# A segment-mean graph layer: gathers of 128 successive edges, with a one-hot in a band of 32 columns

## The chip, the cores and the metric

The kernel runs on one core of a Trainium2 chip. Its time is the device time of one execution in microseconds (us). The runs before give a median of 25,311.82 us (three runs, 25,302.51 to 25,315.38). One execution was taken by the hardware profiler; all rows and lines shown are from it.

## The reference

100,000 nodes with 64 features each, and 3,300,000 edges `(src, dst)`, sorted by `dst`. Of the edges 3,200,000 have random ends (1,600,000 pairs in both directions) and 100,000 are self loops, so a node has 33 edges on the mean, and at least one.

```
h = maximum(layernorm(x), 0)
y = concat([h[dst], h[src] - h[dst]]) @ W.T + b          # one row per edge
out = x + segment_sum(y, dst) / max(count(dst), 1)
```

The matrix product is linear, so the kernel needs for each node only the sum of `h[src]` over its edges and their number; the product with W is done on nodes.

## The kernel before

**First stage** (0 to about 430 us). The normalized features `h` are written to HBM as three bf16 parts that add up to the float32 value, with two columns of ones behind: a row of `h3` has 194 bf16 numbers. The tensor `acc` (a row of 64 sums and a count per node) is set to zero. The function `bounds` (line 249) reads the `dst` numbers of the chunks (see below) and finds for each chunk the least and the greatest node.

**Sorted sets.** The first 2,039,808 edges (256 lists of 7,968) are sorted on VectorE and ScalarE by source node (436 to some 2,500 us for most of it), and are then summed without gathers: for every stretch of 640 nodes a table of `h3` rows is loaded, and TensorE picks rows from it by a one-hot `gh` (line 806) and adds them up by a one-hot `dh` (lines 828 and 836). There are 64 sets; 4 run in a straight part and 60 in a loop of 3 turns with 20 sets each (line 944).

**Chunks.** The last 1,260,192 edges are cut into 352 chunks of 3,584 edges (`CHUNK` = 128 x `J`, `J` = 28). 351 are full; the last has 2,208 edges and 1,376 fills, whose source is node 0 and whose `dst` is V = 100,000, a row behind the last node. Each chunk takes 28 gathers: GpSimd's indirect DMA fetches 128 rows of `h3`, one per partition, into `nb` (line 403). A one-hot `hot` says for each of the 128 gathered rows to which of the 128 nodes from the chunk's least node on it belongs; VectorE writes it for 14 gathers in one instruction (`one_hot`, line 345), by comparing `near`, the node number relative to the least one, four times repeated, with the numbers 0 to 127. TensorE adds up the chunk with 28 matmuls (line 408) into one PSUM tile `ps`, VectorE reduces it to `sums` (lines 420 and 422), and SP stores it in `acc`. In the arrays `src_p` and `dst_p` a chunk has the shape 128 x 28, so that gather `j` takes the edges `j`, `j + 28`, `j + 56` and so on, and partition `p` holds 28 successive edges. The instructions of the chunks are interleaved by hand with those of the sets: 70 chunks with the sort and the first 4 sets, 94 with each turn of the main loop.

**Flags.** The sums in `acc` hold only if the data meet some conditions: a chunk spans under 128 nodes, a list spans under 256 nodes, and so on. Each condition writes a flag into the tensor `odd`. At the end the greatest of all flags is taken (`worst`, line 990), and the two counts in `turns` come from it (lines 995 and 996): `n_clear`, 0 or 1, and `n_slow`, 0 or `NF` = 1,612. They are the number of turns of two loops that follow:

- Line 1004: 28 DMAs set `acc` to zero.
- Line 1014: each turn takes 2,048 edges of the whole list, in the order of the list, sorted or in chunks alike. It loads their numbers (`si`, `di`, and `dr`, which is `dst` in all partitions), gathers 16 times 128 rows (line 1024), compares all `dst` within each gather (`same`), adds up equal ones by a matmul (line 1042), and adds the sums into `acc` with 16 indirect DMAs that accumulate (line 1046). Rows that are not the first of their node go to rows behind the last node.

Before these loops three accumulating stores (line 960) and five accumulating indirect DMAs (line 971) add to `acc` what chunks and lists share at their ends. **Last stage:** the mean, the product with W, and `out` (lines 1057 to 1086).

The part of `bounds` that the change touches, before:

```
nc.vector.tensor_reduce(least[:n, m:m + 1], d[:n], axis=AX.X, op=ALU.min)
if m == NMT - 1:
    nc.vector.scalar_tensor_tensor(d[:n], d[:n], float(V), d[:n], op0=ALU.is_lt, op1=ALU.mult)
nc.vector.tensor_reduce(most[:n, m:m + 1], d[:n], axis=AX.X, op=ALU.max)
```

`NMT` is 3: the chunks are looked at in groups of 128, 128 and 96, one chunk per partition. The multiplication in the last group sets the fills' numbers to 0.

Of the kernel before, what the change touches and what calls it, by code (L numbers as in the profile page):

```python
# [13 lines left out]
F32 = mybir.dt.float32  # L14
BF16 = mybir.dt.bfloat16
I32 = mybir.dt.int32
I16 = mybir.dt.int16
AF = mybir.ActivationFunctionType
ALU = mybir.AluOpType
AX = mybir.AxisListType  # L20
# [7 lines left out]
P = 128  # L28
P = 128
EPS = 1e-5  # L30
J = 28
CHUNK = P * J
# [5 lines left out]
JH = 14  # L38
LAG = 3
GATHER = 1250  # L40
STEP = 1300
GAP = 4
EARLY = 3
EXTRA = 350
KEEP = 5
# [16 lines left out]
D = 4  # L62
# [35 lines left out]
def gnn_preln(ctx: ExitStack, tc, x, src_w, dst_w, src_p, dst_p, src_a, dst_a, wT, b, out, V, E):  # L98
# [17 lines left out]
    nc = tc.nc  # L116
# [3 lines left out]
    CE = C3 + 1  # L120
# [14 lines left out]
    NMT = -(-NCH // P)  # L135
# [27 lines left out]
                   allow_small_or_imprecise_dtypes=True)  # L163
# [7 lines left out]
    for i in range(2):  # L171
# [7 lines left out]
                   allow_small_or_imprecise_dtypes=True)  # L179
# [9 lines left out]
    odd = consts.tile([P, 4 + 5 * LANES], F32, name="odd")  # L189
# [12 lines left out]
    with tc.tile_pool(name="c16s", bufs=1) as c16s:  # L202
        c16_s = c16s.tile([P, REACH + CH], I16, name="c16_s")
        nc.gpsimd.iota(c16_s[:, :REACH].rearrange("p (b s) -> p b s", b=NR), pattern=[[P, NR], [0, P]], base=0,
                       channel_multiplier=1)
# [6 lines left out]
    with tc.tile_pool(name="pre", bufs=2) as pre, tc.tile_pool(name="small", bufs=4) as small, \  # L212
# [13 lines left out]
        for r in range(R, RT, P):  # L226
            n = min(P, RT - r)
# [14 lines left out]


        least = small.tile([P, NMT], F32, name="least", bufs=1)
        most = small.tile([P, NMT], F32, name="most", bufs=1)
        nc.vector.memset(least, 0.0)
        nc.vector.memset(most, 0.0)

        def bounds(m):
            n = min(P, NCH - m * P)  # L250
            d = pre.tile([P, CHUNK], I32, name="d")
            nc.sync.dma_start(d[:n], dst_p[m * P:m * P + n].rearrange("c p j -> c (p j)"))
            nc.vector.tensor_reduce(least[:n, m:m + 1], d[:n], axis=AX.X, op=ALU.min)
            if m == NMT - 1:

                nc.vector.scalar_tensor_tensor(d[:n], d[:n], float(V), d[:n], op0=ALU.is_lt, op1=ALU.mult)
            nc.vector.tensor_reduce(most[:n, m:m + 1], d[:n], axis=AX.X, op=ALU.max)
            if m < NMT - 1:
                return
            span = small.tile([P, NMT], F32, name="span", bufs=1)  # L260
            nc.vector.tensor_sub(span, most, least)
            nc.vector.tensor_reduce(odd[:, 0:1], span, axis=AX.X, op=ALU.max)
            nc.vector.tensor_scalar(odd[:, 0:1], odd[:, 0:1], float(P), None, op0=ALU.is_ge)
            l_ps = pre_ps.tile([NMT, P], F32, name="l_ps")
            nc.tensor.transpose(l_ps, least, ident)
            l_f = small.tile([NMT, P], F32, name="l_f", bufs=1)
            nc.vector.tensor_copy(l_f, l_ps)
            l_i = small.tile([NMT, P], I32, name="l_i", bufs=1)
            nc.vector.tensor_copy(l_i, l_ps)
            nc.sync.dma_start(base_i, l_i)  # L270
            nc.sync.dma_start(base_r, base_i.rearrange("m p -> (m p)")[None, :])
            nc.sync.dma_start(base_f, l_f)
            nc.sync.dma_start(base_b, base_f.rearrange("m p -> (m p)")[None, :].to_broadcast([P, NMT * P]))


        for t in range(0, NPT, T):
# [22 lines left out]
            for u in range(0, T, SUB):  # L299
                n = min(SUB, T - u)  # L300
# [18 lines left out]
    with tc.tile_pool(name="rows", bufs=6) as rows, \  # L319
# [20 lines left out]
        def add_now(all_of_them=False):  # L340
            while later and (all_of_them or (later[0][0] <= count[0] and count[0] - count[1] >= GAP)):
                later.pop(0)[1]()
                count[1] = count[0]

        def one_hot(out, numbers, n):

            shape = [out.shape[0], out.shape[1], n // D, D]
            nc.vector.tensor_tensor(out.rearrange("p k (a d) -> p k a d", d=D),  # L348
                                    numbers[:, :, None].to_broadcast(shape),
                                    upto[:shape[0], :n].rearrange("p (a d) -> p a d", d=D)[:, None].to_broadcast(shape),  # L350
                                    ALU.is_equal)

        def chunks(first, n, dynamic=None):


            def load(q):
                k = min(KG, n - q)
                at = slice(first + q, first + q + k) if dynamic is None else ds(dynamic + q, k)
                si = index.tile([P, KG, J], I32, name="si")
                nc.sync.dma_start(si[:, :k], src_p[at].rearrange("k p j -> p k j"))  # L360
                di = index.tile([P, KG, J], I32, name="di")
                nc.sync.dma_start(di[:, :k], dst_p[at].rearrange("k p j -> p k j"))
                rel = index.tile([P, KG, J], F32, name="rel", bufs=1)
                nc.vector.tensor_sub(rel[:, :k], di[:, :k], base_b[:, at][:, :, None].to_broadcast([P, k, J]))
                near = index.tile([P, KG, J, D], I16, name="near")
                nc.vector.tensor_scalar(near[:, :k], rel[:, :k, :, None].to_broadcast([P, k, J, D]), float(2 * CH), None,
                                        op0=ALU.min)
                return si, near

            def keep(q, sums):  # L370
                c = ds(first + q if dynamic is None else dynamic + q, 1)
                after = ds(first + q + 1 if dynamic is None else dynamic + q + 1, 1)

                def put():
                    at = number(base_r[0:1, c], SP, V)
                    last[SP] = nc.sync.dma_start(acc[ds(at, P)], sums)

                def shared():
                    at = number(base_r[0:1, after], SP, V)
                    last[SP] = nc.sync.dma_start(side_c[c], acc[ds(at, 1)])  # L380

                add_later((LAG - 1) * J, put)
                add_later((LAG - 1) * J + GAP, shared)

            ahead = load(0)
            before = None
            parts = J // JH
            for k in range(n * parts + 1):
                q, part = divmod(k, parts)
                u = q % KG  # L390
                if q < n:
                    if u == 0 and part == 0:
                        si, near = ahead
                    hot = rows.tile([P, JH, P], BF16, name="hot", bufs=4)
                    nb = rows.tile([P, JH, CT], BF16, name="nb")
                    with behind():
                        one_hot(hot, near[:, u, part * JH:part * JH + JH], P)
                if before is not None and before[2] == 0:
                    ps = rows_ps.tile([P, CE], F32, name="ps")
                for j in range(JH):  # L400
                    if q < n:
                        at = part * JH + j
                        last[POOL] = nc.gpsimd.indirect_dma_start(  # L403
                            out=nb[:, j], out_offset=None, in_=h3,
                            in_offset=bass.IndirectOffsetOnAxis(ap=si[:, u, at:at + 1], axis=0))
                        count[0] += 1
                    if before is not None:
                        nc.tensor.matmul(ps, lhsT=before[0][:, j], rhs=before[1][:, j, :CE],  # L408
                                         start=before[2] == 0 and j == 0, stop=before[2] == parts - 1 and j == JH - 1)
                    if q < n:  # L410
                        add_now()
                        yield
                if u == KG - 2 and part == parts - 1 and q + 2 < n:
                    with behind():
                        ahead = load(q + 2)
                if before is not None and before[2] == parts - 1:
                    own = dynamic is None and before[3] < EARLY
                    sums = (few if own else rows).tile([P, C1], F32, name="early" if own else "sums", bufs=EARLY if own else LAG + 2)
                    with behind():
                        nc.vector.tensor_reduce(sums[:, :C], ps[:, :C3].rearrange("p (s c) -> p c s", s=3),  # L420
                                                axis=AX.X, op=ALU.add)
                        nc.vector.tensor_copy(sums[:, C:], ps[:, C3:])  # L422
                    if own:
                        early.append(sums)
                    else:
                        keep(before[3], sums)
                if q < n:
                    before = (hot, nb, part, q)
            add_now(True)
# [325 lines left out]
        def quads(base, n, kept=None):  # L755
# [110 lines left out]
            def keep(u, i, sums):  # L866
# [11 lines left out]
                add_later((LAG - 1) * J, put)  # L878
                add_later((LAG - 1) * J + GAP, shared)

# [16 lines left out]
        with tc.tile_pool(name="few", bufs=1) as few:  # L897
# [14 lines left out]
            with tc.tile_pool(name="keys", bufs=2) as big, tc.tile_pool(name="piece", bufs=2) as piece, \  # L912
                    tc.tile_pool(name="fill", bufs=2) as fill, tc.tile_pool(name="sort_ps", bufs=2, space=PSUM) as ps:
                for l in range(NL):
                    rest = fill_lane(l - 1, fill, took) if l else iter(())
                    for i, ns in enumerate(sort_lane(l, big.tile([P, WL], F32, name="keys"), piece, few, ps)):
                        k = i - 40
# [8 lines left out]
            with tc.tile_pool(name="load", bufs=3) as load, tc.tile_pool(name="hots", bufs=3) as hots, \  # L926
# [13 lines left out]
                for k in range(0, NTB, KEEP):  # L940
                    m = min(TG, NCB - k * TG)
# [20 lines left out]
    with tc.tile_pool(name="few", bufs=1) as few, tc.tile_pool(name="w_ps", bufs=1, space=PSUM) as wps:  # L962
# [18 lines left out]
        small = few.tile([1, 4], F32, name="small")  # L981
# [26 lines left out]
    with tc.tile_pool(name="any", bufs=2) as edge, tc.tile_pool(name="any_c", bufs=1) as one, \  # L1008
# [3 lines left out]
        before = one.tile([P, P], F32, name="before")  # L1012
        nc.vector.tensor_scalar(before, iota, pcol, None, op0=ALU.is_lt)
        with tc.For_i(0, n_slow, 1) as c:
# [25 lines left out]
            for j in range(JA):  # L1040
                ps = edge_ps.tile([P, CE], F32, name="ps")
# [8 lines left out]
    with tc.tile_pool(name="post", bufs=2) as post, tc.tile_pool(name="post_ps", bufs=2, space=PSUM) as post_ps:  # L1050
# [10 lines left out]
        for t in range(0, NPT, T):  # L1061
# [12 lines left out]
            for u in range(0, T, SUB):  # L1074
                n = min(SUB, T - u)
# [50 lines left out]
```

## Time and profile before

| | us |
|---|---|
| median of three runs | 25,311.82 |
| profiled execution | 25,318.98 |
| its span, first to last instruction | 25,317.3 |
| PE (matmul) busy | 14,841.3 (59%) |
| DVE (VectorE) busy | 11,321.0 (45%) |
| POOL (GpSimd) busy | 10,302.7 (41%) |
| ACT (ScalarE) busy | 6,060.7 (24%) |
| mean granted TensorE clock | 0.723 |

Engines run side by side, each in its own order, and wait for each other by semaphores. A row of the page names the line, the engine, the operation, output and input with their shapes, how often it ran, its busy time, the mean of one in ns, and the idle time of the engine just before it with what ended most of it. A line of the timeline gives the start, the duration, and in brackets the idle time before. "SPq" and "POOLq" are queues of engines that issue DMAs; an issue is not the transfer, which ends later.

### The profile page before, as it was taken

The page shows a single profiled execution, that of the slowest core. Times are in us where ns is not written, and L with a number is a line of the kernel's source. Part 1 is how long each engine was busy: PE and PEld are TensorE (multiplying, and loading weights), DVE is VectorE, ACT ScalarE, POOL GpSimd, SP SyncE. Part 2 cuts the span into 40 slices and gives each one's busy share as a digit, 9 for nine tenths or more (in the row PEclk, how much of TensorE's full clock was granted, in tenths as well). Part 3 has the DMA queues.
Part 4 walks back from the last instruction along what each step waited for, and adds up shares of the span by engine and source line. Part 5 has one row for each costly group of instructions (what it writes and reads, how often), then busy time and mean ns, then how long its engine had stood idle before and what let it go on. Part 6 is the DMA issues. An engine that isn't in the chain of part 4 may idle for free. (4 is left out here: it accounts for less than half of the span.)

```text
span 25317.3 us, 562905 instructions
## 1 busy us (share of the span) xinstructions
PE 14841.3 (59%) x238778; PEld 10732.9 (42%) x238778; DVE 11321.0 (45%) x15478; ACT 6060.7 (24%) x11710; POOL 10302.7 (41%) x10609
## 2 busy tenths in 40 slices
PE   4100365466666666665666666666566666666666
PEld 3000244344444444444444444444444444444445
DVE  6878443243444444443444444444344444444444
ACT  4333221122222222221222222222222222222222
POOL 5666533433333333334333333333333333333334
PEclk6555577677777777777777777777777777777777
DMA  6722354354454454454444544444445444444446
GB/s 227 102 46 46 100 172 147 108 151 143 145 149 145 147 149 143 149 153 134 147 143 147 149 146 148 149 147 145 138 144 148 145 150 146 150 145 145 148 145 231
DMA packets 1671411, 3615.08 MB, mean 143 GB/s; under 512 B 951932, under 2 KB 960263, under 8 KB 1663911
## 3 DMA queue, kind: packets, MB, share of 16 engines
q1 hardware_dynamic: 1225338, 3006.63, 36.6%
q0 software_dynamic: 335040, 507.40, 10.5%
q10 hardware_dynamic: 108492, 64.90, 1.3%
q8 instruction: 1874, 30.70, 0.5%
q14 instruction: 667, 5.46, 0.1%
HBM read 3397.56 MB, written 219.36 MB: 143 GB/s over the span
## 5 line engine op out<-in xcount | busy, mean ns | idle before, releaser
L403 POOL DMA_INDIRECT nb<-h,si x9856 | 9337.3, 947 | 13259.9 <-PE ps L408 8539.2
L348 DVE TENSOR_TENSOR dh<-dt,c 128x1024 bf16<-128x1024 int16 x5056 | 3450.9, 683 | 12561.4 <-remote 7908.4
L830 ACT CAST gs<-gp 128x386 bf16<-128x386 f32 x10048 | 4786.8, 482 | 16980.7 <-remote 9615.5
L836 PE MATMUL total<-gs,dh 32*128 32x193 bf16 x160768 | 6254.9, 264 | 4279.4 <-issue 4266.3
L828 PE MATMUL gp<-tab,gh 128*128 128x193 bf16 x48408 | 6076.5, 270 | 2426.6 <-issue 2187.6
L828 PEld LDWEIGHTS <-gh 128*128 128x128 bf16 x60288 | 5384.1, 105 | 4772.8 <-issue 4394.3
L836 PEld LDWEIGHTS <-dh 32*128 32x128 bf16 x160768 | 3875.8, 99 | 6281.3 <-issue 6228.6
L806 DVE TENSOR_TENSOR gh<-srs,c 128x1536 bf16<-128x1536 int16 x5056 | 4760.5, 942 | 15.0 <-issue 7.9
L408 PE MATMUL ps<-nb,hot 128*128 128x193 bf16 x9856 | 1934.7, 281 | 2839.1 <-DVE sums L422 1230.1
L408 PEld LDWEIGHTS <-hot 128*128 128x128 bf16 x9856 | 1048.8, 111 | 3031.1 <-DVE sums L422 1261.7
L828 PE MATMUL gp<-kept,gh 128*128 128x193 bf16 x11880 | 1551.9, 274 | 505.0 <-issue 493.1
L470 ACT COPY tmp<-keys 128x1536 f32<-128x1536 f32 (+14 forms) x540 | 649.6, 1212 | 1324.0 <-DVE keys L472 602.4
L348 DVE TENSOR_TENSOR hot<-near,c 128x1792 bf16<-128x1792 int16 x704 | 759.5, 1079 | 113.6 <-remote 107.4
L471 DVE TENSOR_TENSOR keys<-tmp,keys 128x1536 f32<-128x1536 f32 (+14 forms) x540 | 756.6, 1420 | 88.8 <-ACT junk L548 41.4
L472 DVE TENSOR_TENSOR keys<-tmp,keys 128x1536 f32<-128x1536 f32 (+14 forms) x540 | 756.3, 1419 | 22.4 <-issue 7.1
L795 POOL DMA_INDIRECT rows_x<-h,xs x128 | 120.8, 944 | 985.0 <-DMA xs<-xs_d 930.5
L651 POOL DMA_INDIRECT kf<-ksort,at_i x322 | 306.6, 952 | 205.8 <-ACT k L692 108.3
L856 DVE SCALAR_TENSOR_TENSOR whole<-own,whole 128x193 f32<-128x193 bf16 x512 | 190.3, 413 | 88.3 <-ACT whole L852 87.8
L420 DVE TENSOR_REDUCE sums<-ps 128x64 f32<-128x192 f32 x349 | 122.1, 350 | 209.5 <-remote 197.0
L310 PE MATMUL o_ps<-w_own,hT 128*128 128x128 f32 x784 | 186.7, 376 | 14.4 <-ACT hT L305 13.8
L310 PEld LDWEIGHTS o_ps<-w_own,hT 128*128 128x128 f32 x784 | 154.8, 251 | 77.8 <-ACT hT L305 68.2
L736 POOL DMA_INDIRECT kx<-ksort,xat x128 | 120.7, 943 | 88.5 <-DVE xat L733 43.5
(184 smaller groups left out, 3297.5 us busy)
## 6 DMA issues: line engine op xcount, KB each, us to landing
tab<-tables SPq DMA_DIRECT2D x2668, 727.5 KB
srs<-sr_d SPq DMA_DIRECT2D x1216, 512.0 KB
nb<-h,si POOLq DMA_INDIRECT x9856
tables<-h ACTq DMA_DIRECT2D x157, 242.5 KB
h<-parts SPq DMA_DIRECT2D x28, 1358.0 KB
acc<-zeros SPq DMA_DIRECT2D x28, 910.0 KB
at<-acc SPq DMA_DIRECT2D x28, 910.0 KB
xt<-in_x SPq DMA_DIRECT2D x28, 896.0 KB
```

The costliest lines, as they stand in the source:

```text
L310: nc.tensor.matmul(o2[:, i], lhsT=hT[:, i], rhs=w_own.rearrange("p a c -> p (a c)"), start=False, stop=True)
L348: nc.vector.tensor_tensor(out.rearrange("p k (a d) -> p k a d", d=D), numbers[:, :, None].to_broadcast(shape), upto[:shape[0], :n].rearran ...
L403: last[POOL] = nc.gpsimd.indirect_dma_start(out=nb[:, j], out_offset=None, in_=h3, in_offset=bass.IndirectOffsetOnAxis(ap=si[:, u, at:at + ...
L408: nc.tensor.matmul(ps, lhsT=before[0][:, j], rhs=before[1][:, j, :CE], start=before[2] == 0 and j == 0, stop=before[2] == parts - 1 and j ...
L470: last[ACT] = nc.scalar.copy(tmp, lo)
L471: nc.vector.tensor_tensor(lo, tmp, hi, ALU.min)
L472: last[DVE] = nc.vector.tensor_tensor(hi, tmp, hi, ALU.max)
L651: last[POOL] = nc.gpsimd.indirect_dma_start(out=kf[:, c], out_offset=None, in_=ksort, in_offset=bass.IndirectOffsetOnAxis(ap=at_i[:, c0 + ...
L806: nc.vector.tensor_tensor(gh[:, :m].rearrange("p c i b s -> p (c i) b s"), srs[u, s // SL][:, c:c + m].rearrange("p c i s -> p (c i) s")[: ...
L828: nc.tensor.matmul(gp[:, i], lhsT=ghots[t][:, i, b], rhs=row[:, b + i * (NB - NR), :CE], start=b == 0, stop=b == NR - 1)
L830: nc.scalar.copy(gs[t], gp)
L836: nc.tensor.matmul(total[:, i, to(b)], lhsT=hot[at, b * P:b * P + P], rhs=of[at], start=flags.get("start", False) and b == 0, stop=flags.g ...
```

## The change

It has four parts.

1. `src_p` and `dst_p` are transposed on the host, so that gather `j` of a chunk takes 128 successive edges, `128 j` to `128 j + 127`. With 33 edges a node, these lie on about four nodes around node `4 j` of the chunk.
2. The one-hot of a gather is computed for 32 columns only, those of the nodes `4 j - 16` to `4 j + 15` of the chunk. They are written into a buffer that was set to zero once, at a step of 132 columns, and the matmul reads 128 columns at a step of 128, so that the band moves by four columns from one gather to the next. There are four such buffers, two for each half of a chunk, where there were four of `hot` before.
3. `load` subtracts `4 j - 16` from the relative node numbers.
4. The condition on a chunk in `bounds` is now that all its numbers lie in the band: `off[:, 0]`, the greatest `d - 4 j` less the least node, and `off[:, 1]`, the least node less the least `d - 4 j`, less 1, are to be under 16.

```
+        drift_i = small.tile([P, J], I32, name="drift_i", bufs=1)
+        nc.gpsimd.iota(drift_i, pattern=[[D, J]], base=0, channel_multiplier=0)
...
             nc.vector.tensor_reduce(least[:n, m:m + 1], d[:n], axis=AX.X, op=ALU.min)
+            e = pre.tile([P, CHUNK], I32, name="e", bufs=1)
+            nc.vector.tensor_tensor(e[:n].rearrange("c (p j) -> c p j", j=J), d[:n].rearrange("c (p j) -> c p j", j=J),
+                                    drift_i[:n, None, :].to_broadcast([n, P, J]), ALU.subtract)
+            nc.vector.tensor_reduce(off[:n, 1, m:m + 1], e[:n], axis=AX.X, op=ALU.min)
             if m == NMT - 1:
 
-                nc.vector.scalar_tensor_tensor(d[:n], d[:n], float(V), d[:n], op0=ALU.is_lt, op1=ALU.mult)
-            nc.vector.tensor_reduce(most[:n, m:m + 1], d[:n], axis=AX.X, op=ALU.max)
+                nc.vector.scalar_tensor_tensor(e[:n], d[:n], float(V), e[:n], op0=ALU.is_lt, op1=ALU.mult)
+            nc.vector.tensor_reduce(off[:n, 0, m:m + 1], e[:n], axis=AX.X, op=ALU.max)
             if m < NMT - 1:
                 return
-            span = small.tile([P, NMT], F32, name="span", bufs=1)
-            nc.vector.tensor_sub(span, most, least)
-            nc.vector.tensor_reduce(odd[:, 0:1], span, axis=AX.X, op=ALU.max)
-            nc.vector.tensor_scalar(odd[:, 0:1], odd[:, 0:1], float(P), None, op0=ALU.is_ge)
+            nc.vector.tensor_sub(off[:, 0], off[:, 0], least)
+            nc.vector.tensor_sub(off[:, 1], least, off[:, 1])
+            nc.vector.tensor_scalar_add(off[:, 1], off[:, 1], -1.0)
+            nc.vector.tensor_reduce(odd[:, 0:1], off.rearrange("p i m -> p (i m)"), axis=AX.X, op=ALU.max)
+            nc.vector.tensor_scalar(odd[:, 0:1], odd[:, 0:1], float(BAND // 2), None, op0=ALU.is_ge)
...
+        drift = index.tile([P, J], F32, name="drift", bufs=1)
+        nc.gpsimd.iota(drift, pattern=[[D, J]], base=-(BAND // 2), channel_multiplier=0,
+                       allow_small_or_imprecise_dtypes=True)
...
+                nc.vector.tensor_sub(rel[:, :k], rel[:, :k], drift[:, None, :].to_broadcast([P, k, J]))
...
+            narrow = [[few.tile([P, JH * (P + D) + JH * D], BF16, name=f"hot{part}{i}") for i in range(2)]
+                      for part in range(J // JH)]
+            for hot in narrow[0] + narrow[1]:
+                nc.vector.memset(hot, 0.0)
...
-                    hot = rows.tile([P, JH, P], BF16, name="hot", bufs=4)
+                    hot = narrow[part][q % 2]
                     nb = rows.tile([P, JH, CT], BF16, name="nb")
                     with behind():
-                        one_hot(hot, near[:, u, part * JH:part * JH + JH], P)
+                        one_hot(hot[:, part * JH * D:][:, :JH * (P + D)].rearrange("p (k x) -> p k x", x=P + D)[:, :, :BAND],
+                                near[:, u, part * JH:part * JH + JH], BAND)
...
-                        nc.tensor.matmul(ps, lhsT=before[0][:, j], rhs=before[1][:, j, :CE],
+                        nc.tensor.matmul(ps, lhsT=before[0][:, BAND // 2 + j * P:BAND // 2 + j * P + P], rhs=before[1][:, j, :CE],
...
+    def by_gather(a):
+        return np.ascontiguousarray(a.reshape(nch, J, P).transpose(0, 2, 1))
...
-        "src_p": padded(src[n:], nch * CHUNK, 0).reshape(nch, P, J),
-        "dst_p": padded(dst[n:], nch * CHUNK, V).reshape(nch, P, J),
+        "src_p": by_gather(padded(src[n:], nch * CHUNK, 0)),
+        "dst_p": by_gather(padded(dst[n:], nch * CHUNK, V)),
```

More of the change, by code (lines that the diff above doesn't have):

```diff
@@ L42 @@
 GAP = 4
+BAND = 32
 EARLY = 3
@@ L244, in gnn_preln @@
         least = small.tile([P, NMT], F32, name="least", bufs=1)
[L245 removed]
+        off = small.tile([P, 2, NMT], F32, name="off", bufs=1)
         nc.vector.memset(least, 0.0)
[L247 removed]
+        nc.vector.memset(off, 0.0)
+        drift_i = small.tile([P, J], I32, name="drift_i", bufs=1)
+        nc.gpsimd.iota(drift_i, pattern=[[D, J]], base=0, channel_multiplier=0)
         def bounds(m):
```

## The prediction

> **What bounds the kernel now.** I read the page first, then the timeline of the main loop, then everything that touches the flags `odd` and `turns`, because the diff edits not only the one-hot but the test that decides whether the kernel's last loop runs. From the page's groups (columns: busy us, mean ns | idle before):
>
> ```profile
> span 25317.3 us, 562905 instructions
> ...
> L403 POOL DMA_INDIRECT nb<-h,si x9856 | 9337.3, 947 | 13259.9 <-PE ps L408 8539.2
> L348 DVE TENSOR_TENSOR dh<-dt,c 128x1024 bf16<-128x1024 int16 x5056 | 3450.9, 683 | 12561.4 <-remote 7908.4
> ...
> L348 DVE TENSOR_TENSOR hot<-near,c 128x1792 bf16<-128x1792 int16 x704 | 759.5, 1079 | 113.6 <-remote 107.4
> ```
>
> The kernel spends its time in the main loop (4,592 to 24,965 us), where bursts of gathers and stretches of matmuls alternate; VectorE is 41% busy there. The one-hot that the change narrows costs 759.5 us of VectorE in all, 3% of the span: that is the most the edit can win. The other half of the diff has no such ceiling. The instructions that write or read `turns`:
>
> ```profile
> L996 DVE TENSOR_SCALAR turns<-w_all x1: 131/131/131, 24968.4 to 24968.4; 1x1 int32<-1x1 f32 x1
> ...
> L999 SPq TENSOR_LOAD <-turns x1: 268/268/268, 24969.3 to 24969.3; - x1
> ```
>
> `turns` holds the counts of the two last loops. In the run of before no row of lines 1006 to 1048 exists: the count was zero. What one turn would cost has to come from neighbours. The nearest are the closing scatter-adds of L971, which are the same instruction as the one on L1046 (128 rows of 65 floats added into `acc`), and ordinary gathers. The timeline of the closing part, then of a boundary between two turns of the main loop, then of its first gathers (start, us, engine; in brackets the idle time before and what ended it):
>
> ```profile
> 24974.45 1.61 POOL L971 DMA_INDIRECT acc<-side,side_at  x1 [1.94 <-DMA acc<-early]
> 24977.94 1.58 POOL L971 DMA_INDIRECT acc<-side,side_at  x1 [1.88 <-DMA acc<-side,side_at]
> 24981.96 1.57 POOL L971 DMA_INDIRECT acc<-side,side_at  x1 [2.45 <-issue]
> 24985.44 1.54 POOL L971 DMA_INDIRECT acc<-side,side_at  x1 [1.91 <-DMA acc<-side,side_at]
> 24989.37 1.54 POOL L971 DMA_INDIRECT acc<-side,side_at  x1 [2.39 <-issue]
> ```
>
> ```profile
> 11372.43 0.93 SPq L380 DMA_DIRECT2D side_c<-acc  x1
> 11376.38 0.41 SPq L360 DMA_DIRECT2D si<-in_src_p  x1
> ...
> 11380.04 0.94 POOL L403 DMA_INDIRECT nb<-h,si  x1 [121.08 <-DMA si<-in_src_p]
> ...
> 11381.29 0.94 POOL L403 DMA_INDIRECT nb<-h,si  x1 [0.30 <-issue]
> ```
>
> See: a scatter-add into `acc` waits until the one before has landed, so they start 3.49, 4.02, 3.48 and 3.93 us apart, mean 3.73. Gathers do not wait for each other: 1.25 us apart. A turn's end costs 3.02 us (11373.36 to 11376.38) and its first index load 3.66 us to the first gather (3.34 at the loop's entry, 4592.63 to 4595.97).
>
> **The change part by part.** *The test.* Edges: 3,300,000. The sorted sets take 256 x 7,968 = 2,039,808; chunks take 1,260,192 = 351 x 3,584 + 2,208. So chunk 351 has 2,208 edges and 1,376 fills whose node is V = 100,000. Before, the test compared `most - least` with 128, and fills were masked out of `most`. Now it also takes the minimum of `d - 4j` over the chunk, and takes it before the mask is applied. A fill in gather 27 gives 100,000 - 108 = 99,892. The least node of chunk 351 is 99,932 by the reference's inputs (33 edges a node, 2,208 / 33 = 67 nodes from the end). `off` there is 99,932 - 99,892 - 1 = 39, and 39 >= BAND/2 = 16. The flag is set by the padding, not by an edge: over all 352 chunks the edges themselves leave the drift by at most 7 below and 6 above, so the band holds them and the fast path's sums are sound; the test says otherwise. It also doesn't hang on the seed: the fills always lie at the end, and the last chunk's least node is always some 67 below V.
>
> The VectorE page of the Trainium skill (VectorE: DVE Perf Modes, Specifications) says that integer operands are converted to floats, exact only below 2^24; by that 39 is no rounding artefact. No row of before shows it.
>
> *What the flag starts.* `worst` = 1, so `n_clear` = 1 and `n_slow` = NF = ceil(3,300,000 / 2,048) = 1,612. `acc` is cleared and all edges are summed again after the whole fast path has run. The clear writes 28 x 910 KB = 25.5 MB; at the 326 GB/s of the last slices 78 us, at the 102 of a poor slice 250; I take 100.
>
> *One turn.* Gathers and scatter-adds share GpSimd's queue, and each turn ends in the all-engine boundary. 3.5 (index load, mean of 3.34 and 3.66) + 16 x 1.25 = 20.0 (gathers) + 15 x 3.73 = 56.0 and 1.57 (scatter-adds) + 3.0 (boundary) = 84.0 us. VectorE's work lies beside the gathers: the broadcast `dr` is 1 MB (the 512 KB `srs` issued at 11377.62 released `gh` at 11383.20, 5.6 us; twice that is 11); then `same` and `prior` over 2,048 columns at 1.22 us per 1,024 (row L458, int32), the reduce at 3.88 us per 3,584 (row L253), small operations: together some 8, done at 19 us, and the last gather is issued at 23.5. Cover 4 us; gone, each us late costs 1.6 ms. The 16 matmuls and `sums` (0.35 us, row L420) follow the gathers one by one, a little each, and are hidden by the 3.73 us between scatter-adds.
>
> Sum: 1,612 x 84.0 = 135,400 us; with 25,319 of the profiled execution (span 25,317.3) and 100 for the clear, 160,800. The other edits subtract about 40 (next part). The median of the runs is 7 us below the profiled execution, so nothing more is corrected.
>
> Bounds of the unknown turn. Low: scatter-adds as close as the accumulating stores of L960 (24965.77 to 24968.69, 2.92 apart, the last 0.85): 3.34 + 20 + 15 x 2.92 + 0.85 + 3.0 = 71.0, in all 139,900. High: each scatter-add at 4.02, and a gather as dear as a scatter-add's 1.57 + 0.30: 3.66 + 29.9 + 60.3 + 1.61 + 3.4 = 98.9, in all 184,800. I take 3.73, since L971 is the same operation on the same tensor.
>
> The page DMA: Bandwidth & Descriptors (Anatomy of one DMA) gives 2.0 us plus bytes over 436 GB/s for a GpSimd DMA: 2.08 us for the scatter-add's 33,280 bytes. With 16 x 2.08 in place of 57.6 the turn would be 59.7 and the whole an estimated 121,700. The rows say 3.73, because busy time and landing follow each other; the sum uses the rows.
>
> *The fast path.* The one-hot goes from 1,792 to 448 columns. From 1,024 columns (683 ns) and 1,792 (1,079 ns): 0.516 ns a column, so 386 ns, 0.69 us less each. In the sort (436 to 2,500 us, VectorE 84% busy) lie 84 of them: 58 us. In the main loop 564: 390 us of VectorE, hidden, for the pairs of columns there start 2.07 us apart with a `hot` between and without; priced at nothing, at most 390 less. Added: 45 subtractions of `drift` at 0.39 us (row L364), one more pass over a chunk's 3,584 columns in each of the three calls of `bounds`, 3.9 us each by row L253 (12, in the first stage), 16 memsets of at most 1.6 us. Net in this path: about -40, between -430 and +50. Matmuls, gathers, their count and bytes stay.
>
> **The rivals.** *The flag stays clear* (I misread the mask or the padding). Then only the fast path counts: 25,270, between 24,880 and 25,360. For: the band does hold every edge. Against: the arithmetic above needs only the order of two instructions. It decides at one point: `off` of chunk 351 under 16 instead of 39. This one ends on the other side.
>
> *The loop runs, but scatter-adds don't wait for each other.* Turn: 3.5 + 20 + 16 x 1.87 + 2.2 (landing) + 3.0 = 58.6; in all 119,900. For: the gathers show that GpSimd needs no wait of its own. Against: every L971 row has about 2 us of idle before it.
>
> *The fast path becomes slower by itself*, by strided band writes: at worst 704 x 1.08 = 760 more, under a hundredth of the forecast; it changes no sign and is within the range.
>
> **How the numbers follow.** Forecast (flag set, chained turns) 0.90; unchained 0.04; flag clear 0.06. The time is the forecast's, 160,800. The range is that of its turn, 140,000 to 185,000; it leaves out the two rivals and little else. A measurement of this kernel tells about 0.2% (50 us) from no change: the clear flag's 0.06 divides into 0.04 faster and 0.02 the same; slower 0.94.
>
> **What would show it.** In the profile after: rows of L1006 x28 and of the loop's gathers and scatter-adds, 16 x 1,612 = 25,792 of each, GpSimd's chain of scatter-adds ending the run; up to the end of the main loop nearly the old timeline, with `hot` at 128x448 and about 0.39 us. Scatter-adds starting 3.5 to 4.0 us apart confirm the price; a first scatter-add that waits for VectorE shows the cover gone. If no such rows exist, the reading of the test is wrong, and with it the forecast.

## The result, and the profile after

| us | before | after |
|---|---|---|
| median of four runs | 25,307.17 (25,299.2 to 25,315.38) | 171,124.27 (171,120.03 to 171,135.9) |
| span of the profiled execution | 25,317.3 | 171,122.6 |
| mean granted TensorE clock | 0.723 | 0.533 |
| `turns` written at | 24,968.4 | 24,960.3 |

The changed kernel takes 6.762 times as long (95% interval 6.750 to 6.774), 145,817 us more. The forecast was 160,800 with a range of 140,000 to 185,000: the direction and the mechanism came as forecast, the time is 10,324 us above it. The experiments further on come from four sets of runs, in which the kernel before took 15,431.91, 15,426.68, 25,554.72 and 25,334.20 us, so each kernel is compared only with the kernel before of its own set.

The page of the kernel after (first its span and GpSimd's busy tenths in 40 equal slices, then groups: busy us, mean ns | idle us before, what ended most of it):

```profile
span 171122.6 us, 896608 instructions
...
POOL 5333334444444444444444444444444444444444
...
L1064 POOL DMA_INDIRECT acc<-sums,ti x25792 | 40201.7, 1559 | 56719.9 <-ACT sums L1063 44947.0
L1042 POOL DMA_INDIRECT nb<-h,si x25792 | 31049.5, 1204 | 17846.2 <-DMA si<-in_src_a 10478.1
...
L421 POOL DMA_INDIRECT nb<-h,si x9856 | 9345.4, 948 | 13200.8 <-PE ps L426 8521.3
```

The rows of L1064 and L1042 had no counterpart before. Their number, 25,792, is 16 x 1,612: the last loop ran all its turns. Busy and idle time of the two together are 145,817 us, as much as the loss, because GpSimd's queue carries the loop from one end to the other. The gathers of the main loop (L421, L403 before) cost what they did: 948 ns against 947, and an idle time of 13,200.8 us against 13,259.9.

The group of the narrowed one-hot, and the instruction that writes `turns` (its start is the fourth figure from the left):

```profile
L360 DVE TENSOR_TENSOR hot<-near,c 128x448 bf16<-128x448 int16 x704 | 268.0, 381 | 113.4 <-remote 100.5 <-PE ps L426 12.8
```

```profile
L1014 DVE TENSOR_SCALAR turns<-w_all x1: 131/131/131, 24960.3 to 24960.3; 1x1 int32<-1x1 f32 x1
```

```profile
L1024 ACTq DMA_DIRECT2D acc<-zeros x28: 338/376/1292, 24986.5 to 25032.8; - x28
```

`hot` takes 381 ns where it took 1,079; VectorE has 491.5 us less of it. The fast path reaches its flags 8.1 us earlier than before, a sixtieth of that. Then, in the third fence, the clear of `acc` starts.

One turn of the loop, from the timeline of the kernel after (start, us, engine and line, idle time before it and what ended it; SPq is SyncE's DMA queue):

```profile
90064.08 1.55 POOL L1064 DMA_INDIRECT acc<-sums,ti  x1 [2.37 <-DMA acc<-sums,ti]
90069.59 0.33 SPq L1034 DMA_DIRECT2D si<-in_src_a  x1
...
90072.25 1.03 POOL L1042 DMA_INDIRECT nb<-h,si  x1 [6.62 <-DMA si<-in_src_a]
...
90074.86 3.56 DVE L1046 TENSOR_TENSOR same<-dr,di 128x2048 bf16<-128x2048 int32 x1
90074.87 0.94 POOL L1042 DMA_INDIRECT nb<-h,si  x1 [0.30 <-issue]
90076.12 3.08 POOL L1042 DMA_INDIRECT nb<-h,si  x1 [0.30 <-issue]
90078.45 2.29 DVE L1049 TENSOR_TENSOR prior<-same,before 128x2048 f32<-128x2048 bf16 x1
...
90079.50 2.06 POOL L1042 DMA_INDIRECT nb<-h,si  x1 [0.30 <-issue]
90080.93 2.28 DVE L1051 TENSOR_REDUCE first<-prior 128x16 f32<-128x2048 f32 x1
90081.87 0.94 POOL L1042 DMA_INDIRECT nb<-h,si  x1 [0.31 <-issue]
...
90084.08 0.23 DVE L1057 TENSOR_SCALAR ti<-to,aside 128x16 int32<-128x16 f32 x1
...
90095.60 1.62 POOL L1064 DMA_INDIRECT acc<-sums,ti  x1 [0.30 <-issue]
90099.58 1.58 POOL L1064 DMA_INDIRECT acc<-sums,ti  x1 [2.36 <-ACT sums L1063]
```

The first row is the last scatter-add of the turn before; from its end (90,065.63) to the next turn's first load lie 3.96 us. Three readings follow. The first scatter-add of the turn starts 0.30 us after the last gather with "issue" for a reason: VectorE, done with `ti` at 90,084.31, is not what it waits for. Next, two gathers that run beside `same` and `prior`, 3.08 and 2.06 us, are longer than the 0.94 of those beside the reduction. They end 0.78 and 0.82 us after VectorE's instruction has ended (at 90,078.42 and 90,080.74), while the gather that starts 0.01 us after `same` still takes 0.94.

The third reading is about the wait between scatter-adds. The group puts their idle time down mostly to ACT's copy into `sums`. The answer for line 1064 alone (idle us, times):

```profile
  ACT sums L1063: 44947.0, 19344
  DMA acc<-sums,ti: 11281.8, 4836
```

`sums` has four buffers. The reduction of line 1062 waits for a landing because that frees a buffer, and it and the copy then fill this buffer for a scatter-add that comes three places after the next one. The last three waits of each turn (3 x 1,612 = 4,836) have no reduction or copy beside them and are put down to the landing itself; they last 2.33 us each, the others 2.32. So it is the landing of the scatter-add before that sets the pace, and the copy only ends at about the same time.

### The profile page after: what moved, and what is told of

The parts are those of the page before. It is cut to its first block, busy times and chain, and to the rows that moved or that the text cites. A ratio compares the mean times of both kernels' runs of the same rounds, so it can differ in the third digit from the quotient of the medians.

```text
span 171122.6 us, 896608 instructions
## 1 busy us (share of the span) xinstructions
PE 22930.1 (13%) x264570; PEld 13385.7 (8%) x264570; DVE 33251.9 (19%) x52623; ACT 10163.4 (6%) x37502; POOL 81568.4 (48%) x62195
## 5 line engine op out<-in xcount | busy, mean ns | idle before, releaser
L1064 POOL DMA_INDIRECT acc<-sums,ti x25792 | 40201.7, 1559 | 56719.9 <-ACT sums L1063 44947.0
L1042 POOL DMA_INDIRECT nb<-h,si x25792 | 31049.5, 1204 | 17846.2 <-DMA si<-in_src_a 10478.1
L1060 PE MATMUL ps<-nb,same 128*128 128x193 bf16 x25792 | 8092.4, 332 | 137719.2 <-DVE same L1046 66465.0
L1062 DVE TENSOR_REDUCE sums<-ps 128x64 f32<-128x192 f32 x25792 | 9159.7, 356 | 87136.7 <-DMA acc<-sums,ti 87136.4
L421 POOL DMA_INDIRECT nb<-h,si x9856 | 9345.4, 948 | 13200.8 <-PE ps L426 8521.3
L1060 PEld LDWEIGHTS <-same 128*128 128x128 bf16 x25792 | 2666.3, 109 | 143141.5 <-DVE same L1046 73037.6
L1063 ACT COPY sums<-ps 128x1 f32<-128x1 f32 x25792 | 4105.4, 159 | 141747.4 <-DVE sums L1062 141315.4
L1046 DVE TENSOR_TENSOR same<-dr,di 128x2048 bf16<-128x2048 int32 x1612 | 5742.2, 3562 | 0.0
L1049 DVE TENSOR_TENSOR prior<-same,before 128x2048 f32<-128x2048 bf16 x1612 | 3694.7, 2292 | 55.5
L1051 DVE TENSOR_REDUCE first<-prior 128x16 f32<-128x2048 f32 x1612 | 3669.2, 2276 | 0.0
L489 DVE TENSOR_TENSOR keys<-tmp,keys 128x1536 f32<-128x1536 f32 (+14 forms) x540 | 757.4, 1421 | 120.4 <-issue 59.4
```

The lines of the kernel that those rows point to most:

```text
L421: last[POOL] = nc.gpsimd.indirect_dma_start(out=nb[:, j], out_offset=None, in_=h3, in_offset=bass.IndirectOffsetOnAxis(ap=si[:, u, at:at + ...
L1042: nc.gpsimd.indirect_dma_start(out=nb[:, j], out_offset=None, in_=h3, in_offset=bass.IndirectOffsetOnAxis(ap=si[:, j:j + 1], axis=0))
L1046: nc.vector.tensor_tensor(same, dr.rearrange("q p j -> q j p"), di[:, :, None].to_broadcast([P, JA, P]), ALU.is_equal)
L1049: nc.vector.tensor_mul(prior, same, before[:, None, :].to_broadcast([P, JA, P]))
L1060: nc.tensor.matmul(ps, lhsT=same[:, j], rhs=nb[:, j, :CE], start=True, stop=True)
L1063: nc.scalar.copy(sums[:, C:], ps[:, C3:])
```

## The experiments

### Padding alone sets the flag: e1_fill_far

```
-        "dst_p": by_gather(padded(dst[n:], nch * CHUNK, V)),
+        "dst_p": by_gather(padded(dst[n:], nch * CHUNK, V + P)),
```

> The changed kernel with one constant altered: the 1,376 fills of the last chunk carry node V + 128 instead of V, so that a fill less 4j can never fall below the chunk's least node. Theory: the padding alone set the flag. Then both closing loops run zero turns, no rows of lines 1024 and 1042 exist, and what is left is the fast path alone. In the profile of the changed kernel its flags are ready at 24,960.3 us, against 24,968.4 before, so about 25,299 us (25,250 to 25,340). Rival: an edge outside the band, or another condition, set the flag: 171,120 us as before the edit. For the fast path there are two more views: my prediction's sum (25,270) and VectorE's whole saving of 0.69 us x 704 (24,820).

Measured: 15,415.09 us against 15,431.91 of before, ratio 0.9986 (0.9976 to 0.9996). (The expectation's 25,299 counts on a before of 25,307; e10, the same kernel in such a set, took 25,332.) No turn of the last loop ran:

```profile
span 15416.3 us, 562941 instructions
...
L421 POOL DMA_INDIRECT nb<-h,si x9856 | 9356.5, 949 | 4323.7 <-issue 2840.7
```

It has 333,667 instructions fewer than the kernel after, with the same band, the same test and the same edges. What differs is the number in 1,376 fills of one chunk. So the flag came from the padding, and none of the real edges leaves the band. The loss is not a price of the narrow one-hot. Without the loop the band kernel wins 17 us of 15,432, with an interval (6 to 37 us) that only just leaves out no change; in e10 it is 2 us, with no change inside the interval.

### The fast path's first stage: e2_least_of_four

E1, and the least node of a chunk is looked for in its first four gathers alone:

```
-            nc.vector.tensor_reduce(least[:n, m:m + 1], d[:n], axis=AX.X, op=ALU.min)
+            nc.vector.tensor_reduce(least[:n, m:m + 1], d[:n].rearrange("c (p j) -> c p j", j=J)[:, :, :BAND // 2 // D],
+                                    axis=AX.XY, op=ALU.min)
```

> As e1_fill_far, and the least node of a chunk is taken over its first four gathers only (512 of 3,584 columns; the other edges are held by the band test). Theory: the first stage is bound by VectorE there, and the two additional passes of bounds (e, and its minimum) explain why the first gather came at 458.9 us instead of 436.1. Three reduces fall from 3.88 us to about 0.7, so the first gather comes some 10 us earlier than in e1_fill_far (449) and the time is 10 us less. Rival: the first stage is bound by something else (stores of h, the clearing of acc): no difference between the two.

Measured: 15,414.45 us, ratio 0.9990 (0.9979 to 1.0002), the same as e1. The three reductions took 0.68 us instead of 3.88, so some 10 us of VectorE went and nothing of it shows in the time; 10 us is 0.06% of this kernel. The traces tell more: the first gather starts at 453.3 us where e1 has 459.4 (in executions with the same first stage it agrees within 1.3 us). So some 6 of the 10 us arrive at the end of the first stage: VectorE is on its path, as the theory said, though not for all of the time.

### The loop without any of the change: e3_before_flagged

The kernel before, its flag set by hand:

```
-            nc.vector.tensor_scalar(odd[:, 0:1], odd[:, 0:1], float(P), None, op0=ALU.is_ge)
+            nc.vector.tensor_scalar(odd[:, 0:1], odd[:, 0:1], float(P // 2), None, op0=ALU.is_ge)
```

> The kernel before with one constant altered: the limit on a chunk's span is 64 nodes instead of 128, which sets the flag. No band, no transposed arrays. Theory: all of the loss is the closing loops, and nothing of it is the band: 1,612 turns of 90.1 us and the clear come on top of the unchanged fast path, so 171,132 us (8 us over the changed kernel's 171,124), within 60. Rival: the band, the buffers or the order of the edges make the closing loop dearer or cheaper: a difference over 150 us.

Measured: 162,945.81 us, which is 147,514 more than before in the same set. Turns of 91.48 us (162,535.5 less 15,168.3, over 1,611). The loss of the change appears in full without the band. It lies 201 us above e5, the kernel after in the second set, and the expectation had called a difference of more than 150 a sign of the rival. These are single runs of two sets. The gathers' busy time accounts for 109 us of it (31,085.5 against 30,976.3) and the scatter-adds' idle time for 59; what makes either is open. The 201 us are 0.14% of the loss.

### Why gathers cost more than 1.25 us: e4_psum_operands

The kernel after, with one operand of `same` and one of `prior` in PSUM:

```
-        before = one.tile([P, P], F32, name="before")
+        before = edge_ps.tile([P, P], F32, name="before", bufs=1)
...
+            dp = edge_ps.tile([P, JA], I32, name="dp", bufs=1)
+            nc.vector.tensor_copy(dp, di)
...
-                                    di[:, :, None].to_broadcast([P, JA, P]), ALU.is_equal)
+                                    dp[:, :, None].to_broadcast([P, JA, P]), ALU.is_equal)
```

> The changed kernel with the small operands of same and prior (the 16 numbers of di, and the 128 x 128 of before) in PSUM instead of SBUF. In the changed kernel's turn at 90,069 us the gather that starts beside same takes 3.08 us, the one beside prior 2.06, the one beside the reduce first 0.94; the mean of the loop's gathers is 1,204 ns. Theory: an indirect DMA's issue on GpSimd waits while VectorE runs an instruction with two SBUF operands. Then all gathers take about 0.95 us, the turn falls from 90.1 to 86 to 87 us and the time to 165,500 (164,500 to 166,500). The Trainium skill (SBUF - State Buffer, Who interferes with whom) states such a rule: a VectorE instruction with two SBUF inputs contends with GpSimd instructions that read SBUF. Rival: the slow gathers come from the 1 MB broadcast dr or from the transfers themselves: mean still 1.20 us, time 171,100 to 171,500.

Measured: 156,423.01 us, 6,322 less than e5, the kernel after in a set with the same time before (next section). The timeline of e4 and then the group of its gathers:

```profile
90005.53 3.55 DVE L1048 TENSOR_TENSOR same<-dr,dp 128x2048 bf16<-128x2048 int32 x1
90006.66 0.94 POOL L1042 DMA_INDIRECT nb<-h,si  x1 [0.30 <-issue]
90007.91 0.95 POOL L1042 DMA_INDIRECT nb<-h,si  x1 [0.30 <-issue]
90009.12 2.29 DVE L1051 TENSOR_TENSOR prior<-same,before 128x2048 f32<-128x2048 bf16 x1
...
90009.16 0.94 POOL L1042 DMA_INDIRECT nb<-h,si  x1 [0.30 <-issue]
```

```profile
L1042 POOL DMA_INDIRECT nb<-h,si x25792 | 24567.7, 953 | 18019.4 <-DMA si<-in_src_a 10650.5
```

VectorE's two instructions take as long as before, but the gathers beside them are back at 0.94 us: 953 ns on the mean instead of the 1,201 of e5:

```profile
L1042 POOL DMA_INDIRECT nb<-h,si x25792 | 30976.3, 1201 | 18017.7 <-DMA si<-in_src_a 10649.5
```

The turn is 87.43 us against 91.36 there: 3.93 less, close to 16 x 0.248 = 3.97. (The expectation's 164,500 to 166,500 us counted on a before of 25,307.) The broadcast `dr` and the transfers are as they were, so the rival is out: the gathers are slow beside these two instructions only while both of their operands lie in SBUF. The main loop agrees: the second operand `c` of its one-hots lies in PSUM (pool `cps`), VectorE is busy for 15.58 of 20 us in the stretch of e1 shown at the end, and e1's gathers there take 949 ns on the mean. The Trainium skill's page "SBUF — State Buffer", under "Who interferes with whom", says that a VectorE instruction with two SBUF inputs contends with a GpSimd instruction that reads SBUF; the 3.08 and 2.06 us of after and the 0.94 of e4 agree.

### The kernel after beside the faster before: e5_after_again

No edit.

> The changed kernel, unaltered, beside the other kernels of this call: the chip of the first four experiments ran the kernel before in 15,432 us, not 25,307, so a changed kernel on the same chip is wanted to compare them with. Theory: the loss is 1,612 turns of the closing loop, whatever the chip does in the main loop. So the time is the kernel before plus 145,800 to 147,600 us: on that chip 162,900 (as e3_before_flagged, 162,946, within 80), on the first chip 171,120. Rival: the loss scales with the chip, 6.76 times 15,432 = 104,300.

Measured: 162,744.56 us, that is 147,318 over its own before. That lies within the forecast of 145,800 to 147,600 for the loss, and rules out the rival's 104,300; it is 201 us below e3, where 80 had been allowed. Turns of 91.36 us ((162,330.5 - 15,151.8) / 1,611). The loop costs nearly the same, 147,318 against 145,817, whether the part ahead of it takes 15 or 25 ms. Of the 1,501 between the two, 1,420 stand as idle time ahead of the scatter-adds (58,140.0 against 56,719.9), 0.055 us each; why is open.

### The chain of scatter-adds: e6_two_targets

The kernel after with a second tensor beside `acc`, which every other scatter-add goes to (what lands in `acc2` is left out of the sums at the end, so this is a kernel for timing only):

```
+    acc2 = dram.tile([R, C1], F32, name="acc2")
...
-                    out=acc, out_offset=bass.IndirectOffsetOnAxis(ap=ti[:, j:j + 1], axis=0),
+                    out=acc2 if j % 2 else acc, out_offset=bass.IndirectOffsetOnAxis(ap=ti[:, j:j + 1], axis=0),
```

> The changed kernel; the scatter-adds of a turn go alternately to acc and to a second tensor acc2 (also cleared; it is left out of the sums at the end). Theory: a scatter-add starts only when the one before into the same tensor has landed, 3.9 us apart; with two targets two such chains run side by side, and starts are 1.9 to 2.1 us apart. The turn falls from 90.4 to 91.5 by 15 x 1.9 = 28 us to some 62 to 63, and the time by 46,000 us: about 117,000 on the chip of the first four experiments, 125,000 on the first chip. Rival: an accumulating indirect DMA occupies GpSimd's queue until it has landed, whatever its target: the turn is unchanged, and the time at most 100 us more (the second clear).

Measured: 115,094.1 us, 47,650 less than e5. From its timeline:

```profile
60024.09 1.62 POOL L1066 DMA_INDIRECT acc<-sums,ti  x1 [0.30 <-issue]
60026.02 1.58 POOL L1066 DMA_INDIRECT acc<-sums,ti  x1 [0.30 <-issue]
60028.17 1.56 POOL L1066 DMA_INDIRECT acc<-sums,ti  x1 [0.57 <-ACT sums L1065]
```

The group on its page:

```profile
L1066 POOL DMA_INDIRECT acc<-sums,ti x25792 | 40213.4, 1559 | 10541.7 <-ACT sums L1065 8197.1
```

The instruction is as long as it was (1.56 us), the idle time ahead of it has fallen from 58,140.0 us in e5 to 10,541.7, and the starts lie 1.98 us apart instead of 3.94. The turn is 61.76 us. So GpSimd can issue one in 2 us; what holds it to 3.9 is that two accumulations into the same tensor wait for each other's landing. Two into the same tensor start 3.96 us apart here too: there are now two such chains side by side.

### What the one-hot's time on VectorE is worth: e7 to e12

Kernels of this group change only how often the one-hot is written. E7 and e12 are the kernel before with `hot` written twice; e9 and e11 are e1 with the band written twice; e8 is the kernel before as it is, and e10 is e1 again.

```
                         one_hot(hot, near[:, u, part * JH:part * JH + JH], P)
+                        one_hot(hot, near[:, u, part * JH:part * JH + JH], P)
```

> The kernel before, with every one-hot hot written twice: 704 x 1.08 = 760 us more of VectorE, the opposite of what the change takes away (0.70 x 704 = 490). Theory: VectorE's time for hot is hidden, in the main loop behind gathers and matmuls, and for the larger part in the sort: the time grows by 0 to 100 us. Rival: VectorE is on the path: 400 to 760 us more, which would mean that the narrow one-hot wins 260 to 490 and loses it again elsewhere.

> The kernel before, unaltered, for a profile on the chip of the other experiments, to lay beside e1_fill_far's stage by stage. Theory: the two differ in the first stage (first gather some 23 us earlier here, for the changed bounds makes two more passes of 3.9 us over each of three groups), and the narrow one-hot gives back some 40 us behind it, most of it in the sort (436 to some 3,100 us), where VectorE is 84% busy. Rival: what is given back comes from the main loop.

> e1_fill_far with every band one-hot written twice: VectorE has 2 x 0.38 = 0.76 us per hot, between e1_fill_far (0.38; 15,415 us) and the kernel before (1.08; 15,427 to 15,432), where e7_hot_twice had 2.16 (15,731). Theory: about 1.1 us per hot are covered by other work, and what lies above is paid: 15,415 to 15,435, no difference to e1_fill_far beyond 20 us. Rival: each us of VectorE costs 0.4 us, as between the kernel before and e7_hot_twice (304 of 760): 0.4 x 0.38 x 704 = 107 us more than e1_fill_far.

> e1_fill_far once more, beside the next two in one call: the calls so far found the kernel before at 15,430 us (two calls) or at 25,310 to 25,555 us (two calls, on one of the same chips), so kernels of different calls can't be laid side by side. Theory (VectorE's time per hot is covered up to about 1.1 us): ratio to the kernel before 0.997 to 1.000. Rival (the narrow one-hot pays in full): 490 us less, 0.968 to 0.981.

> e9_band_twice once more, in the same call as the other two. Theory of the cover: within 20 us of e10_fill_far_2. Rival (each us of VectorE costs 0.4 us): 107 us above it.

> e7_hot_twice once more, in the same call. Where the kernel before takes 15,430 us: 304 us more, as measured. Where it takes 25,310 to 25,555 us: the main loop stands still for VectorE half the time (41% busy), the cover is larger, and the theory gives 0 to 100 us more, most of it in the sort; the rival, that VectorE's time is paid for at the same rate, 300 us more.

| run | VectorE, change for the one-hot | its before | time | ratio (95%) |
|---|---|---|---|---|
| e1_fill_far | -492 | 15,431.91 | 15,415.09 | 0.9986 (0.9976 to 0.9996) |
| e7_hot_twice | +762 | 15,426.68 | 15,730.81 | 1.0206 (1.0190 to 1.0221) |
| e8_before_here | 0 | 25,554.72 | 25,563.63 | one run |
| e9_band_twice | -218 | 25,554.72 | 25,567.75 | 1.0007 (0.9998 to 1.0016) |
| e10_fill_far_2 | -492 | 25,334.20 | 25,332.01 | 0.9999 (0.9990 to 1.0008) |
| e11_band_twice_2 | -219 | 25,334.20 | 25,350.45 | 1.0006 (0.9997 to 1.0015) |
| e12_hot_twice_2 | +762 | 25,334.20 | 25,414.85 | 1.0033 (1.0022 to 1.0044) |

The second column is the busy time of the row of `hot` on each kernel's page less the 759.5 us of before; for e7 from this row:

```profile
L348 DVE TENSOR_TENSOR hot<-near,c 128x1792 bf16<-128x1792 int16 x1408 | 1521.1, 1081 | 73.6 <-PE ps L409 57.9
```

Time added is partly paid: 81 us of 762 in e12, as the theory had it, and 304 in e7, which lies between the theory's 0 to 100 and the rival's 400 to 760. Time taken away wins 2 to 17 us of 492 (e10, e1), and with some 219 us away (e9, e11) the kernels are 13 and 16 us above before, within no change. The four band kernels also carry the dearer `bounds`, which starts the first gather some 22 us later, so their totals are net of it. E11 lies 18 us above e10, within the theory's 20 and far from the rival's 107. So most of VectorE's work on `hot` up to its old 1.08 us lies beside other work, and above that it begins to show. E8 and e9 were to be laid beside e1 stage by stage; both came out near 25,560 us, where e1 had 15,415, so they can't be, and e10 to e12 put the question again within one set.

## Why the prediction was right or wrong

**The flag: right.** The prediction said that the fill, not an edge, sets it, and that `off` would be 39 where 16 is the bound. The loop ran; e1 moved the fills and it did not run. The 39 itself comes from the inputs; no run reads it. The rival "the flag stays clear" was priced at 25,270, and the chip's answer to that condition is e10: 25,332 beside 25,334.

**The number of turns, and what ends them: right.** 25,792 gathers and scatter-adds, GpSimd's queue at the end of every turn. The rival of scatter-adds that don't wait for each other gave a turn of 58.6; with two targets, where each has only half of the waits, e6 took 61.76. The rival had a fair price for a kernel that this isn't, partly by luck, since it too counted 20.0 for gathers that took 24.0 there.

**The turn: mis-sized by 6.4 us.** The mean turn is (170,714.2 - 25,051.9) / 1,611 = 90.42 us, times 1,612 a sum of 145,757. The prediction's terms, beside one stretch (from the first scatter-add at 90,005.50 to the next turn's first at 90,095.60) and beside the mean of all turns, taken from the starts and ends in the trace:

| term | predicted | one stretch | mean |
|---|---|---|---|
| index load | 3.5 | 2.66 | 2.55 |
| 16 gathers | 20.0 | 23.35 | 24.14 |
| 15 scatter-adds | 56.0 | 58.58 | 58.27 |
| the last one | 1.57 | 1.55 | 1.55 |
| boundary | 3.0 | 3.96 | 3.91 |
| sum | 84.0 | 90.10 | 90.42 |

The step that failed most is the gathers. "16 x 1.25" took the start-to-start time of a gather with nothing hurtful beside it, and the prediction then placed VectorE's `same` and `prior` beside them as free. They were free for the path of VectorE, not for GpSimd: the gathers are 4.14 us a turn above their term, and e4, which takes the two instructions away from them, is 3.93 us a turn faster than e5, some 6,300 us of the 10,324 missing. The scatter-adds' 3.73 was the mean of four gaps between 3.48 and 4.02; in the loop the mean is 3.88: 2.3 us a turn. The reduction and the copy into `sums` are not the reason, for the last three gaps of a turn, which have neither, are as long (3.89); the reason is open. The boundary, taken from the main loop, is 0.91 short and the load has 0.95 too much; that these two cancel is luck.

The Trainium skill's page "DMA: Bandwidth & Descriptors", under "Anatomy of one DMA", gave the prediction an estimate of 2.08 us per scatter-add. The measured 3.88 us is nearly twice that and decides; e6's 1.98 us is close to it, but only because two chains of 3.96 us run side by side.

**The cover: held, by other numbers.** VectorE was to be done 19 us into the turn, before a last gather at 23.5. It was done at 14.7, before a first scatter-add at 26.0. `dr` arrived within 5.3 us of the loads and not in 11; `same` took 3.56 us and not 2.44 (it reads `dr` with a step of 64 bytes, which may be why; no run tests it); the reduction took 2.28 where 2.2 was worked out. The scatter-adds' idle time of 0.30 us at that place shows it.

**The clear: 67 us where 100 was taken** (memset at 24,984.80, first load of the loop at 25,051.86).

**The fast path: -40 predicted, -8.1 measured, and the parts were further off than the sum.** `hot` was forecast at 386 ns and took 381. But in the sort "84 x 0.69 = 58 us" was counted as won because VectorE is busy there: from the first gather to the loads of the kept tables it took 2,920.4 us (458.9 to 3,379.3) instead of 2,923.9 (436.1 to 3,360.0). So 3.5 of 58 came. The sort did not get shorter by what its VectorE work lost; which other engine holds it was not tested. The other loss is in `bounds`, where "one more pass" was a misreading of the diff. The timeline of the kernel after:

```profile
36.35 6.39 DVE L258 TENSOR_TENSOR e<-d,drift_i 128x3584 int32<-128x3584 int32 x1
42.77 3.89 DVE L260 TENSOR_REDUCE off<-e 128x1 f32<-128x3584 int32 x1
```

There are two more passes in each call, the subtraction and the second reduction. 3.9 to 6.4 us each, three times; the first gather starts 22.8 us later, and e2 shows that most of what VectorE saves there reaches it. The rest of the fast path, from the kept loads to the flags, is 27 us shorter, and no single part of it can be named for that.

The main loop's 390 us, "priced at nothing", were right to be: e10 and e1 win 2 and 17 us in all.

## What to carry to other kernels

A condition that guards a fast path has two prices, and the larger one is that of the way it opens; before changing such a test, put the padding through it as well as the data, and follow the order of mask and reduction line by line. Work hidden beside another engine is free only if it doesn't slow that engine: where GpSimd's gathers set the pace and run beside a VectorE instruction with two SBUF operands, try one of them in PSUM, as e4 did. And a busy engine (VectorE, 84% in the sort) is not a bound: its time is worth something only where another waits for it, which runs with more and with less of the work show better than the share.

## What the runs showed that was not expected

The main loop runs at two speeds, and the kernel's text doesn't decide which. The kernel before took 15.43 ms in two sets and 25.3 to 25.6 in the others; one chip showed both (15,432 in the first set, 25,555 in the third), so the chip alone doesn't decide it. All executions of one set agree, and the kernels of a set stand together: e1 is 15,415 in one and 25,332 (e10) in another. In stretches of 20 us (PE, weight load, VectorE, ScalarE, GpSimd, each with busy us and instructions; then granted clock, DMA share, GB/s), first e8, then e1:

```profile
14920.00:14940.00 20.00, 20.00 (x454) 16.72 (x451) 14.42 (x20) 9.51 (x20) 0.00 (x0) 1.00 0.84 249
14960.00:14980.00 20.00, 3.49 (x11) 0.99 (x10) 1.55 (x2) 0.00 (x0) 12.85 (x14) 0.50 0.19 37
```

```profile
9900.00:9920.00 20.00, 19.94 (x452) 16.57 (x449) 15.58 (x23) 9.64 (x20) 15.12 (x17) 1.00 0.91 301
```

At the lower speed (e8) TensorE and the gathers hardly overlap: 454 matmuls and no gather, then 14 gathers and 11 matmuls. At the higher one (e1), 452 matmuls and 17 gathers share the same 20 us. Within a burst of gathers in before, TensorE starts a matmul only every 0.7 to 1.4 us:

```profile
14959.75 0.34 PE L828 MATMUL gp<-tab,gh 128*128 128x193 bf16 x1 [1.10 <-issue]
14960.46 0.32 PE L828 MATMUL gp<-tab,gh 128*128 128x193 bf16 x1 [0.37 <-issue]
14961.88 0.32 PE L828 MATMUL gp<-tab,gh 128*128 128x193 bf16 x1 [1.09 <-issue]
```

"issue" says that the profile has nothing it waits for, so it seems to have work. The gathers then wait for PE in turn (8,539.2 us before L403 ended by `ps`, as the prediction's page shows). What slows TensorE there is open; no run here was made to settle it. The prediction took this alternation for the kernel's own rhythm. It doesn't touch the result, since the last loop costs 147,318 us beside the one and 145,817 beside the other.
